# Graph attention kernel: rows loaded by SyncE as single tiles of 28 quads instead of as all tiles of 6 quads

## The chip, the cores and the metric

The kernel runs on one core of a Trainium2 chip. The metric is the device time of one execution in microseconds. A core has TensorE (PE in the profile; PEld is its weight load), VectorE (DVE), ScalarE (ACT), GpSimd (POOL) and SyncE (SP), each with an instruction queue of its own that runs in program order, and 16 DMA engines that they share.

## The reference

A graph with 6250 nodes and 206250 edges, sorted by receiver. Each edge has two feature vectors of 32 values, which pass through a small two-layer network each. Every node gets query, key and value rows of 128 values (8 heads of 16). Per edge and head, a score is the sum of query (receiver) times edge weight times key (sender); it scales the sender's value row, and the results are summed by receiver. The sum is added to the node's row and normalized.

```python
w_ij = silu(edge_feats @ rad_W1 + rad_b1) @ rad_W2 + rad_b2
w_ij = w_ij + silu(chi_scalar @ sph_W1 + sph_b1) @ sph_W2 + sph_b2
q_i = (x @ Wq)[receivers]
k_j = (x @ Wk)[senders]
alpha = (q_i * w_ij * k_j).reshape(-1, 8, 16).sum(-1) / sqrt(16) * cutoffs[:, None]
v_j = (x @ Wv)[senders].reshape(-1, 8, 16)
out = segment_sum(alpha[..., None] * v_j, receivers) / 16
return layernorm(x + out.reshape(-1, 128))
```

## The kernel before

**Tiles.** 128 edges are a tile, 4 tiles a quad (512 edges), 4 quads a group (2048 edges). There are 101 groups and 403 quads. `order` (L131) lists the quads as they are worked on: within a group 0, 2, 1, 3. Below, "quad i" is the i-th of that list.

**Prologue.** Key and value rows of all nodes are computed and written to a table `kv_tab` in HBM, 1 KB a node. For the first 10 quads the rows are computed from gathered node rows instead (L241). Then `rows_f` (L388 to L395) turns the sender numbers of chosen quads into byte addresses: VectorE multiplies by 1024, TensorE transposes, and `at_i` holds them as integers, a row of 128 per tile. `bias_rows`, the scaling of the edge weights and then `pick(0)` follow on VectorE in program order, and from `pick(0)` the first group's queries (`turn_q`, `make_q`) are made.

**The sender rows.** Every quad needs 512 rows of the table. Two ways lead there:
- `gathers` (L139), for nearly all quads: GpSimd issues four indirect DMAs, one a tile, each fetching 128 rows by the sender numbers in `src_i`. It is called 14 quads ahead (`AHEAD`). Each gather waits, by an added dependency, for a mark: one of the last four matmuls of `weigh` for quad i, where the gather is for quad i + 14.
- `load_rows` (L150), for 6 quads (`row_quads`, every 65th): SyncE issues 512 DMAs of one row each into a buffer `rows` (two of them). A unit is 16 rows: one instruction loads 16 addresses from `at_i` into registers (L163), then 16 DMAs follow (L167). The 32 units of a quad are spread over the quads before it; they must all be issued 8 quads ahead (`ROW_LEAD`).

**The main loop** (L666) runs over groups and four slots. In slot i TensorE sums messages of the group before (`sum_quads`), makes the first layers of quad i + 2, the queries at the edges of quad i + 1 and the edge weights (`weigh`) of quad i + 1. ScalarE applies the silu. VectorE does `multiply` for quad i + 1, then `scores` and `messages` for quad i.

**SyncE's queue** in one group, in this order: slot 0 an `x` load three groups ahead (a register load at L192 and a DMA at L195, behind a mark of TensorE), slot 2 the features `feats` of the group after next (L172, behind a mark of TensorE) and its relative receivers `relb` (L183), in every slot one `out` write (L624) if a row block is ready, and last in every slot `load_rows`. The writes of `out` overlap in rows, so one waits for the one before it. `feats` of a group is first read by TensorE's first layers two quads ahead of the group; `relb` by VectorE's `one_hots_T` (L432) in slot 1 of the group before.

**The order of work** is written out by hand; nothing moves an instruction within an engine's queue.

Of the kernel before, what the change touches and what calls it, by code (L numbers as in the profile page):

```python
# [12 lines left out]
F32 = mybir.dt.float32  # L13
BF16 = mybir.dt.bfloat16
U8 = mybir.dt.uint8
I32 = mybir.dt.int32
AF = mybir.ActivationFunctionType
OP = mybir.AluOpType
# [3 lines left out]
SP = mybir.EngineType.SP  # L22
WAIT = mybir.DependencyInfo(mybir.DependencyClass.Sync, mybir.DependencyReason.DATA)

P = 128
N = 6250
D = 128
HEADS = 8
HD = D // HEADS
# [3 lines left out]
QT = 4  # L33
# [4 lines left out]
EQ = P * QT  # L38
# [6 lines left out]
ROW_BYTES = 2 * D * 4  # L45
XQ = 10
RING = 16
ROW_QUADS = 6
ROW_LEAD = 8
ROW_UNIT = 16  # L50
CHECK = 20
XL = 3
NEIGHBORS = 16.0
# [5 lines left out]
def gnn_kernel(ctx, tc, x, src, dst, weight, edges, rad_W1, rad_b1, rad_W2, rad_b2,  # L59
# [14 lines left out]
    nc = tc.nc  # L74
    const = ctx.enter_context(tc.tile_pool(name="const", bufs=1))
# [8 lines left out]
    dst_i = const.tile([P, NT], I32, name="dst_i")  # L84
    src_i = const.tile([P, NT], I32, name="src_i")
    src_x = const.tile([P, math.ceil(XQ / NQ) * GT], I32, name="src_x")
    at_i = const.tile([ROW_QUADS * QT, P], I32, name="at_i")
    scale = const.tile([P, NT], F32, name="scale")
    w1 = const.tile([P, D], F32, name="w1")
    w2 = const.tile([P, 2, D], F32, name="w2")  # L90
# [5 lines left out]
    ident = const.tile([P, P], F32, name="ident")  # L96
# [16 lines left out]
    ep = ctx.enter_context(tc.tile_pool(name="edge", bufs=2))  # L113
# [7 lines left out]
    def quad_of(name, bufs, width=D):  # L121
        return ep.tile([P, QT, width], F32, name=name, bufs=bufs)

    def gather(o, table, index):
        return nc.gpsimd.indirect_dma_start(  # L125
            out=o, out_offset=None, in_=table,
            in_offset=bass.IndirectOffsetOnAxis(ap=index, axis=0))
# [1 line left out]


    order = [g * NQ + j for g in range(NG) for j in (0, 2, 1, 3) if g * NQ + j < QUADS]  # L131
    every = (len(order) - ROW_LEAD) // ROW_QUADS
    row_at = [(n + 1) * every for n in range(ROW_QUADS)]
    row_quads = {order[i] for i in row_at}
    r_of = {}
    feats_of, relb_of, act_of, kv_of, hot_of, hotT_of, x_of, q_of, msg_of = ({} for _ in range(9))
    po_of, part_of, to_of, tot_of, xT_of, y0_of, kq_of, pick_of, pq_of, pw_of = ({} for _ in range(10))

    def gathers(q, marks=()):  # L139

        if q in row_quads:
            return
        kv = quad_of("kv", RING, 2 * D)
        for t in range(QT):
            o = gather(kv[:, t, :], kv_tab, src_i[:, q * QT + t:q * QT + t + 1])
            if marks:
                tc.add_manual_dep(o.ins, marks[t].ins.name, WAIT, reason="no gather ahead of TensorE")
        kv_of[q] = kv

    def load_rows(i):  # L150

        k = max(i + ROW_LEAD - 1, 0) // every
        if k >= ROW_QUADS:
            return
        q, start = order[row_at[k]], max(k * every - ROW_LEAD + 1, 0)
        slots, units = row_at[k] - ROW_LEAD + 1 - start, EQ // ROW_UNIT
        a, b = ((j * units + slots - 1) // slots for j in (i - start, i - start + 1))
        if i == start:
            kv_of[q] = quad_of("rows", 2, 2 * D)
        table = kv_tab.bitcast(U8).rearrange("(o n) b -> o (n b)", o=1)  # L160
        for u in range(a, min(b, units)):
            t, e = u * ROW_UNIT // P, u * ROW_UNIT % P
            _, rows = nc.values_load_multi_w_load_instructions(  # L163
                at_i[k * QT + t:k * QT + t + 1, e:e + ROW_UNIT], engines=(SP,), min_val=0,
                max_val=(N - 1) * ROW_BYTES, skip_runtime_bounds_check_because="senders are nodes")
            for p in range(ROW_UNIT):
                nc.sync.dma_start(kv_of[q][e + p:e + p + 1, t, :].bitcast(U8),  # L167
                                  table[:, ds(rows[p], ROW_BYTES)])

    def load_feats(g, mark=None):  # L170
        feats_of[g] = gp.tile([P, EG // 2], F32, name="feats")
        o = nc.sync.dma_start(feats_of[g], edges[g])  # L172
        if mark is not None:
            tc.add_manual_dep(o.ins, mark.ins.name, WAIT, reason="one signal of TensorE a quad")
# [42 lines left out]
    with tc.tile_pool(name="nodes", bufs=1) as nodes, \  # L217
# [167 lines left out]
                nc.sync.dma_start(scale, weight)  # L385
        for q in order[XQ:AHEAD]:
            gathers(q)
        rows_f = nodes.tile([P, ROW_QUADS * QT], F32, name="rows_f")  # L388
        for k, i in enumerate(row_at):
            nc.vector.tensor_scalar(rows_f[:, k * QT:(k + 1) * QT],  # L390
                                    src_i[:, order[i] * QT:(order[i] + 1) * QT],
                                    float(ROW_BYTES), None, op0=OP.mult)
        pt = nps.tile([P, QT, P], F32, name="pt", bufs=3)
        nc.tensor.transpose(pt[:ROW_QUADS * QT, 0, :], rows_f, ident)
        nc.vector.tensor_copy(at_i, pt[:ROW_QUADS * QT, 0, :])  # L395
        nc.vector.tensor_tensor(bsum, b2[:, 0:1], b2[:, 1:2], op=OP.add)
        bias_rows()
        for t in range(P, NT, P):
# [5 lines left out]
    with tc.tile_pool(name="ps", bufs=1, space=PSUM) as pp:  # L404
# [57 lines left out]
        def after(o, mark, reason="one signal of TensorE a quad"):  # L462
            tc.add_manual_dep(o.ins, mark.ins.name, WAIT, reason=reason)

        def behind(o, marks, k):

            if marks:
                after(o, marks[k], "a signal of TensorE behind the quad's own")
# [16 lines left out]
        def weigh(q):  # L485

            pw = pp.tile([P, EQ], F32, name="pw", bufs=2)
            nc.tensor.matmul(pw, onesb, brow.rearrange("p t d -> p (t d)"), start=True, stop=False)  # L488
            pw = pw_of[q] = pw.rearrange("p (t d) -> p t d", d=D)
            marks = []  # L490
            for t in range(QT):
                for i in range(2):
                    o = nc.tensor.matmul(pw[:, t, :], act_of[q, i][:, t * P:(t + 1) * P], w2[:, i, :],  # L493
                                         start=False, stop=(t == QT - 1 and i == 1))
                    marks.append(o)
            return marks

        def multiply(q, mark=None, t=slice(0, QT)):
            if t.start == 0:
                kq_of[q] = quad_of("kq", 3)  # L500
            o = nc.vector.tensor_tensor(kq_of[q][:, t, :], pq_of[q][:, t, :], kv_of[q][:, t, :D],  # L501
                                        op=OP.mult)
            if mark is not None:
                after(o, mark)

        def scores(q, t=slice(0, QT), marks=()):
            n = t.stop - t.start
# [12 lines left out]
        def messages(q, alpha, t=slice(0, QT), marks=()):  # L520

            if t.start == 0:
                msg_of[q] = quad_of("msg", XQ)
            o = nc.vector.tensor_tensor(  # L524
                msg_of[q][:, t, :].rearrange("p t (h e) -> p t h e", e=HD),
                kv_of[q][:, t, D:].rearrange("p t (h e) -> p t h e", e=HD),
                alpha[:, :, :, None].to_broadcast([P, t.stop - t.start, HEADS, HD]), op=OP.mult)
            behind(o, marks, 3)

        def sum_quads(g, t, j=None):  # L530

            if g not in po_of:
                po_of[g] = pp.tile([P, D], F32, name="po")
            for j in range(NQ) if j is None else (j,):
                o = nc.tensor.matmul(po_of[g][j * W:(j + 1) * W, :], hot_of[g][:, j * QT + t, :],  # L535
                                     msg_of[g * NQ + j][:, t, :], start=(t == 0), stop=(t == QT - 1))
            return o

        wides = []

        def wide_one_hots(q):

            t = slice(q * QT, (q + 1) * QT)
            d = gp.tile([P, QT], F32, name="d", bufs=NQ)
            nc.vector.tensor_copy(d, dst_i[:, t])
            nc.vector.tensor_scalar(d, d, gb[:, q // NQ:q // NQ + 1], None, op0=OP.subtract)
            k = order[-3:].index(q)
            if k % 2 == 0:
                wides.append(quad_of("rows", 2, 2 * D).rearrange("p t (h r) -> p h t r", r=P))
            hot_of[q, "wide"] = wides[-1][:, k % 2]  # L550
            nc.vector.tensor_tensor(hot_of[q, "wide"], d[:, :, None].to_broadcast([P, QT, P]),
                                    colp[:, None, :].to_broadcast([P, QT, P]), op=OP.is_equal)

# [110 lines left out]
        marks = weigh(order[0])  # L664
        mark = marks[-1]
        for g in range(NG - 1):  # L666
            for slot, j in enumerate((0, 2, 1, 3)):
                q = g * NQ + j
                i = g * NQ + slot
# [9 lines left out]
                if 1 <= g:  # L679
                    for t in ((), (0, 1), (2,), (3,))[slot]:  # L680
                        mark = sum_quads(g - 1, t)
                first_layers(order[i + 2])
                mark = q_at_edges(order[i + 1])
                marks = weigh(order[i + 1])
# [32 lines left out]
                if g == NG - 2 and slot == 0:  # L717
                    wide_one_hots(order[-1])
                    n = nc.values_load(general, min_val=0, max_val=1)
# [7 lines left out]
        mark = q_at_edges(b)  # L727
        marks = weigh(b)
# [11 lines left out]
        mark = q_at_edges(c)  # L740
        marks = weigh(c)
# [195 lines left out]
```

## Time and profile before

| | |
|---|---|
| median of 3 runs | 2010.27 us (2009.23 to 2012.95) |
| the profiled execution's own time | 2011.89 us |
| its span, first to last instruction | 2010.1 us |
| mean granted clock of TensorE | 0.917 |
| gathers on GpSimd (table / nodes) | 1548 / 40 |
| rows issued by SyncE | 3072 of 1 KB |
| register loads of addresses on SyncE | 192 of 16 |

The profile page gives busy time by engine, the groups of instructions by source line, and the chain of waits followed back from the last instruction. A timeline line has start and duration in us, the engine, the line, the operation, what it writes and reads, how many were merged, and in brackets the idle time of the engine before it with what ended that. A line of a stretch has the stretch, its length, the busy time of the engine with its instructions, TensorE's granted clock, the DMA share and GB/s. Issuing instructions of SyncE are listed as SPq and do not count as busy time.

### The profile page before, as it was taken

To read this page: it belongs to the slowest core of one execution; us is meant where nothing else is said; L and a number is where in the kernel's file an instruction comes from. 1 tells how busy PE (TensorE), PEld (TensorE's weight loads), DVE (VectorE), ACT (ScalarE), POOL (GpSimd) and SP (SyncE) were. 2 spreads that over 40 slices of the span, in tenths; PEclk is the share of its full clock that TensorE was granted. 3 is DMA by queue.
4 is the path that set the end of the run, shared out by engine and by line. 5 is a ranking of instruction groups with operands and counts; after the bars stand their busy time and mean duration, and the time that the engine had idled before them with its cause. 6 is when DMAs were issued, how large, how long until landed. Compare 5 with 4: busy or idle time off the path is not lost.

```text
span 2010.1 us, 50508 instructions
## 1 busy us (share of the span) xinstructions
PE 1811.3 (90%) x16012; PEld 1519.6 (76%) x16012; DVE 1466.5 (73%) x3015; ACT 720.8 (36%) x1426; POOL 1505.3 (75%) x1596
## 2 busy tenths in 40 slices
PE   9898988999998988998998999988889889988897
PEld 7787877877877777777777777777777777777786
DVE  6687777878877776766767677767676776767687
ACT  2343333444343333333333332333332333323333
POOL 7777777777777777777777777777777777777775
PEclk9898988999998998998999889889998998898898
DMA  8454555555555555554554545554545555555553
GB/s 312 131 154 139 157 143 150 157 155 153 156 156 149 147 155 147 148 150 144 156 154 139 153 145 150 143 152 142 154 142 152 152 144 154 143 149 144 151 150 89
DMA packets 146414, 304.45 MB, mean 151 GB/s; under 512 B 36717, under 2 KB 79581, under 8 KB 146141
## 3 DMA queue, kind: packets, MB, share of 16 engines
q0 software_dynamic: 75584, 205.62, 36.6%
q1 hardware_dynamic: 69056, 95.15, 14.8%
q8 instruction: 127, 2.08, 0.4%
q14 instruction: 147, 1.20, 0.2%
q10 hardware_dynamic: 1500, 0.40, 0.1%
HBM read 287.58 MB, written 13.46 MB: 150 GB/s over the span
## 4 chain that ended last, share of the span: by engine, by line
PE 53%; DMA 20%; DVE 11%; issue 6%; ACT 4%; POOL 3%; SPq 2%; DVEq 0%; ACTq 0%; POOLq 0%
PE pw L493 27%; DMA kv<-kv_tab,src_i 17%; PE pq L457 10%; PE ph L446 7%; DVE kq L501 4%; PE po L535 4%; PE pw L488 2%; DMA feats<-in_edges 2%; DVE side L511 2%; DVE kq L509 2%; POOL msg L125 2%; POOL kv L125 1%; SPq L167 1%; ACT L478 1%; ACT y L612 1%
## 5 line engine op out<-in xcount | busy, mean ns | idle before, releaser
L125 POOL DMA_INDIRECT kv<-kv_tab,src_i x1548 | 1465.3, 947 | 474.3 <-PE pw L493 186.0
L478 ACT ACTIVATE act<-ph,b 128x512 f32<-128x512 f32 x806 | 518.4, 685 | 1150.5 <-PE pq L457 1124.0
L493 PE MATMUL pw<-w,act 128*128 128x128 f32 x6448 | 915.1, 300 | 0.0
L493 PEld LDWEIGHTS pw<-w,act 128*128 128x128 f32 x6448 | 834.8, 209 | 105.8 <-issue 93.9
L446 PE MATMUL ph<-feats,w 32*128 32x512 f32 x1612 | 497.2, 676 | 41.0 <-ACT act L478 20.9
L457 PE MATMUL pq<-q,hotT 32*128 32x128 f32 x3224 | 495.8, 296 | 42.6 <-DVE kq L501 42.6
L501 DVE TENSOR_TENSOR kq<-pq,kv 128x512 f32<-128x512 f32 x398 | 273.4, 687 | 331.9 <-DMA kv<-kv_tab,src_i 188.2
L457 PEld LDWEIGHTS pq<-q,hotT 32*128 32x128 f32 x3224 | 416.8, 198 | 79.9 <-issue 50.6
L511 DVE TENSOR_REDUCE side<-kq 128x32 f32<-128x512 f32 x404 | 280.2, 693 | 42.7 <-PE pw L493 0.9
L524 DVE TENSOR_TENSOR msg<-kv,side 128x512 f32<-128x512 f32 x398 | 273.2, 686 | 43.2 <-PE pq L457 0.9
L509 DVE TENSOR_TENSOR kq<-pw,kq 128x512 f32<-128x512 f32 x404 | 274.5, 679 | 0.1
L446 PEld LDWEIGHTS ph<-feats,w 32*128 32x128 f32 x1612 | 136.9, 193 | 123.8 <-issue 80.0
L488 PE MATMUL pw<-brow,onesb 3*128 3x512 bf16 x403 | 161.1, 400 | 0.0
L535 PE MATMUL po<-msg,hot 128*32 128x128 f32 x3200 | 155.7, 292 | 0.0
L574 PE MATMUL pq<-part,to 128*128 128x128 f32 x200 | 46.7, 317 | 82.9 <-DVE kq L501 58.4
L513 DVE TENSOR_TENSOR side<-side,scale 128x32 f32<-128x32 f32 x404 | 80.6, 200 | 42.6 <-DVE side L511 0.5
L574 PEld LDWEIGHTS pq<-part,to 128*128 128x128 f32 x200 | 31.9, 201 | 93.6 <-issue 57.4
L535 PEld LDWEIGHTS po<-msg,hot 128*32 128x32 f32 x3200 | 71.5, 111 | 38.9 <-issue 5.6
L432 DVE TENSOR_TENSOR hotT<-relb,side 128x512 f32<-128x512 bf16 x101 | 68.8, 682 | 34.0 <-DMA relb<-rel_lin 34.0
L437 DVE TENSOR_TENSOR hot<-rel,side 128x512 f32<-128x512 f32 x100 | 66.1, 661 | 0.0
L426 PE MATMUL pq<-wq,xT 128*128 128x128 f32 (+1 forms) x202 | 45.1, 308 | 15.2 <-DVE kq L501 14.4
L125 POOL DMA_INDIRECT msg<-in_x,src_x x40 | 39.0, 976 | 13.5 <-issue 11.6
(107 smaller groups left out, 839.3 us busy)
## 6 DMA issues: line engine op xcount, KB each, us to landing
feats<-in_edges SPq DMA_DIRECT2D x101, 512.0 KB
rows<-kv_tab SPq DMA_DIRECT2D x3072, 1.0 KB
kv<-kv_tab,src_i POOLq DMA_INDIRECT x1548
relb<-rel_lin SPq DMA_DIRECT2D x101, 128.0 KB
x<-in_x SPq DMA_DIRECT2D x101, 64.0 KB
out<-y SPq DMA_DIRECT2D x101, 64.0 KB
kv_tab<-kv SPq DMA_DIRECT2D x12, 512.0 KB
act<-in_x SPq DMA_DIRECT2D x12, 256.0 KB
```

The lines of the kernel that those rows point to most:

```text
L125: return nc.gpsimd.indirect_dma_start(out=o, out_offset=None, in_=table, in_offset=bass.IndirectOffsetOnAxis(ap=index, axis=0))
L446: return nc.tensor.matmul(act_of[q, i], w1[r0:r0 + R, :], feats_of[g][r0:r0 + R, c0:c0 + EQ], start=True, stop=True)
L457: o = nc.tensor.matmul(pq_of[q][:, t, :], hotT_of[g][b, t * P:(t + 1) * P], q_of[g][b, :], start=True, stop=True)
L478: o = nc.scalar.activation(act, act_of[q, i], AF.Silu, bias=b1[:, i:i + 1])
L488: nc.tensor.matmul(pw, onesb, brow.rearrange("p t d -> p (t d)"), start=True, stop=False)
L493: o = nc.tensor.matmul(pw[:, t, :], act_of[q, i][:, t * P:(t + 1) * P], w2[:, i, :], start=False, stop=(t == QT - 1 and i == 1))
L501: o = nc.vector.tensor_tensor(kq_of[q][:, t, :], pq_of[q][:, t, :], kv_of[q][:, t, :D], op=OP.mult)
L509: nc.vector.tensor_tensor(m, pw_of[q][:, t, :], m, op=OP.mult)
L511: o = nc.vector.tensor_reduce(alpha, m.rearrange("p t (h e) -> p t h e", e=HD), AX.X, OP.add)
L513: o = nc.vector.tensor_tensor(alpha, alpha, scale[:, q * QT + t.start:q * QT + t.stop, None].to_broadcast([P, n, HEADS]), op=OP.mult)
L524: o = nc.vector.tensor_tensor(msg_of[q][:, t, :].rearrange("p t (h e) -> p t h e", e=HD), kv_of[q][:, t, D:].rearrange("p t (h e) -> p t h ...
L535: o = nc.tensor.matmul(po_of[g][j * W:(j + 1) * W, :], hot_of[g][:, j * QT + t, :], msg_of[g * NQ + j][:, t, :], start=(t == 0), stop=(t = ...
```

## The change

Instead of all four tiles of 6 quads (24 tiles), SyncE loads the last tile of each of 28 quads (28 tiles), every 14th of the list. GpSimd gathers the other three tiles of those quads. A unit is 32 rows in place of 16, so a tile takes 4 units. The buffer of rows is a quarter of its size. In these quads `multiply` and `messages` run as two instructions each, three tiles from the gathered buffer and one from the other. The prologue makes 28 columns of addresses with one instruction each, where it made 24 with six. The one-hot tables of the last three quads, which used the buffer of rows, get one of their own.

```diff
-ROW_QUADS = 6
+ROW_TILES = 28
 ROW_LEAD = 8
-ROW_UNIT = 16
+ROW_UNIT = 32
...
-    every = (len(order) - ROW_LEAD) // ROW_QUADS
-    row_at = [(n + 1) * every for n in range(ROW_QUADS)]
+    every = (len(order) - ROW_LEAD) // ROW_TILES
+    row_at = [(n + 1) * every for n in range(ROW_TILES)]
...
     def gathers(q, marks=()):
-        if q in row_quads:
-            return
         kv = quad_of("kv", RING, 2 * D)
-        for t in range(QT):
+        for t in range(QT - 1 if q in row_quads else QT):
...
-        q, start = order[row_at[k]], max(k * every - ROW_LEAD + 1, 0)
-        slots, units = row_at[k] - ROW_LEAD + 1 - start, EQ // ROW_UNIT
+        slots, units = row_at[k] - ROW_LEAD + 1 - start, P // ROW_UNIT
         a, b = ((j * units + slots - 1) // slots for j in (i - start, i - start + 1))
         if i == start:
-            kv_of[q] = quad_of("rows", 2, 2 * D)
+            row_of[q] = ep.tile([P, 1, 2 * D], F32, name="rows", bufs=2)
-        for u in range(a, min(b, units)):
-            t, e = u * ROW_UNIT // P, u * ROW_UNIT % P
+        for e in range(a * ROW_UNIT, min(b, units) * ROW_UNIT, ROW_UNIT):
             _, rows = nc.values_load_multi_w_load_instructions(
-                at_i[k * QT + t:k * QT + t + 1, e:e + ROW_UNIT], engines=(SP,), min_val=0,
+                at_i[k:k + 1, e:e + ROW_UNIT], engines=(SP,), min_val=0,
...
+    def kv_parts(q, t):
+        if q not in row_quads:
+            return [(t, kv_of[q][:, t, :])]
+        return [(slice(0, QT - 1), kv_of[q][:, :QT - 1, :]), (slice(QT - 1, QT), row_of[q])]
...
-        rows_f = nodes.tile([P, ROW_QUADS * QT], F32, name="rows_f")
+        rows_f = nodes.tile([P, ROW_TILES], F32, name="rows_f")
         for k, i in enumerate(row_at):
-            nc.vector.tensor_scalar(rows_f[:, k * QT:(k + 1) * QT],
-                                    src_i[:, order[i] * QT:(order[i] + 1) * QT],
+            c = order[i] * QT + QT - 1
+            nc.vector.tensor_scalar(rows_f[:, k:k + 1], src_i[:, c:c + 1],
                                     float(ROW_BYTES), None, op0=OP.mult)
...
-            o = nc.vector.tensor_tensor(kq_of[q][:, t, :], pq_of[q][:, t, :], kv_of[q][:, t, :D],
-                                        op=OP.mult)
+            for u, kv in kv_parts(q, t):
+                o = nc.vector.tensor_tensor(kq_of[q][:, u, :], pq_of[q][:, u, :], kv[:, :, :D],
+                                            op=OP.mult)
...
-            if k % 2 == 0:
-                wides.append(quad_of("rows", 2, 2 * D).rearrange("p t (h r) -> p h t r", r=P))
-            hot_of[q, "wide"] = wides[-1][:, k % 2]
+            hot_of[q, "wide"] = quad_of("wide", 3, P)
```

The units of a tile are spread over the 14 slots between two such quads, and for the first tile over the first 7 slots of the loop: its four units stand in slots 0, 1, 3 and 5, and those of the second in 7, 10, 14 and 17. Before, the first quad's 32 units were spread over 58 slots.

More of the change, by code (lines that the diff above doesn't have):

```diff
@@ L86, in gnn_kernel @@
     src_x = const.tile([P, math.ceil(XQ / NQ) * GT], I32, name="src_x")
-    at_i = const.tile([ROW_QUADS * QT, P], I32, name="at_i")
+    at_i = const.tile([ROW_TILES, P], I32, name="at_i")
     scale = const.tile([P, NT], F32, name="scale")
@@ L131, in gnn_kernel @@
     order = [g * NQ + j for g in range(NG) for j in (0, 2, 1, 3) if g * NQ + j < QUADS]
-    every = (len(order) - ROW_LEAD) // ROW_QUADS
-    row_at = [(n + 1) * every for n in range(ROW_QUADS)]
+    every = (len(order) - ROW_LEAD) // ROW_TILES
+    row_at = [(n + 1) * every for n in range(ROW_TILES)]
     row_quads = {order[i] for i in row_at}
+    row_of = {}
     r_of = {}
@@ L152, in load_rows @@
         k = max(i + ROW_LEAD - 1, 0) // every
-        if k >= ROW_QUADS:
+        if k >= ROW_TILES:
             return
         q, start = order[row_at[k]], max(k * every - ROW_LEAD + 1, 0)
-        slots, units = row_at[k] - ROW_LEAD + 1 - start, EQ // ROW_UNIT
+        slots, units = row_at[k] - ROW_LEAD + 1 - start, P // ROW_UNIT
         a, b = ((j * units + slots - 1) // slots for j in (i - start, i - start + 1))
         if i == start:
-            kv_of[q] = quad_of("rows", 2, 2 * D)
+            row_of[q] = ep.tile([P, 1, 2 * D], F32, name="rows", bufs=2)
         table = kv_tab.bitcast(U8).rearrange("(o n) b -> o (n b)", o=1)
-        for u in range(a, min(b, units)):
-            t, e = u * ROW_UNIT // P, u * ROW_UNIT % P
+        for e in range(a * ROW_UNIT, min(b, units) * ROW_UNIT, ROW_UNIT):
             _, rows = nc.values_load_multi_w_load_instructions(
-                at_i[k * QT + t:k * QT + t + 1, e:e + ROW_UNIT], engines=(SP,), min_val=0,
+                at_i[k:k + 1, e:e + ROW_UNIT], engines=(SP,), min_val=0,
                 max_val=(N - 1) * ROW_BYTES, skip_runtime_bounds_check_because="senders are nodes")
             for p in range(ROW_UNIT):
-                nc.sync.dma_start(kv_of[q][e + p:e + p + 1, t, :].bitcast(U8),
+                nc.sync.dma_start(row_of[q][e + p:e + p + 1, 0, :].bitcast(U8),
                                   table[:, ds(rows[p], ROW_BYTES)])
+    def kv_parts(q, t):
+        if q not in row_quads:
+            return [(t, kv_of[q][:, t, :])]
+        return [(slice(0, QT - 1), kv_of[q][:, :QT - 1, :]), (slice(QT - 1, QT), row_of[q])]
     def load_feats(g, mark=None):
@@ L387, in gnn_kernel @@
             gathers(q)
-        rows_f = nodes.tile([P, ROW_QUADS * QT], F32, name="rows_f")
+        rows_f = nodes.tile([P, ROW_TILES], F32, name="rows_f")
         for k, i in enumerate(row_at):
-            nc.vector.tensor_scalar(rows_f[:, k * QT:(k + 1) * QT],
-                                    src_i[:, order[i] * QT:(order[i] + 1) * QT],
+            c = order[i] * QT + QT - 1
+            nc.vector.tensor_scalar(rows_f[:, k:k + 1], src_i[:, c:c + 1],
                                     float(ROW_BYTES), None, op0=OP.mult)
         pt = nps.tile([P, QT, P], F32, name="pt", bufs=3)
-        nc.tensor.transpose(pt[:ROW_QUADS * QT, 0, :], rows_f, ident)
-        nc.vector.tensor_copy(at_i, pt[:ROW_QUADS * QT, 0, :])
+        nc.tensor.transpose(pt[:ROW_TILES, 0, :], rows_f, ident)
+        nc.vector.tensor_copy(at_i, pt[:ROW_TILES, 0, :])
         nc.vector.tensor_tensor(bsum, b2[:, 0:1], b2[:, 1:2], op=OP.add)
@@ L500, in multiply @@
                 kq_of[q] = quad_of("kq", 3)
-            o = nc.vector.tensor_tensor(kq_of[q][:, t, :], pq_of[q][:, t, :], kv_of[q][:, t, :D],
-                                        op=OP.mult)
-            if mark is not None:
-                after(o, mark)
+            for u, kv in kv_parts(q, t):
+                o = nc.vector.tensor_tensor(kq_of[q][:, u, :], pq_of[q][:, u, :], kv[:, :, :D],
+                                            op=OP.mult)
+                if mark is not None:
+                    after(o, mark)
         def scores(q, t=slice(0, QT), marks=()):
@@ L523, in messages @@
                 msg_of[q] = quad_of("msg", XQ)
[L524 to L528, printed above, removed]
+            for u, kv in kv_parts(q, t):
+                n = u.stop - u.start
+                o = nc.vector.tensor_tensor(
+                    msg_of[q][:, u, :].rearrange("p t (h e) -> p t h e", e=HD),
+                    kv[:, :, D:].rearrange("p t (h e) -> p t h e", e=HD),
+                    alpha[:, u.start - t.start:u.stop - t.start, :, None].to_broadcast(
+                        [P, n, HEADS, HD]), op=OP.mult)
+                behind(o, marks, 3)
         def sum_quads(g, t, j=None):
@@ L537, in sum_quads @@
             return o
-        wides = []
         def wide_one_hots(q):
@@ L546, in wide_one_hots @@
             nc.vector.tensor_scalar(d, d, gb[:, q // NQ:q // NQ + 1], None, op0=OP.subtract)
-            k = order[-3:].index(q)
-            if k % 2 == 0:
-                wides.append(quad_of("rows", 2, 2 * D).rearrange("p t (h r) -> p h t r", r=P))
-            hot_of[q, "wide"] = wides[-1][:, k % 2]
+            hot_of[q, "wide"] = quad_of("wide", 3, P)
             nc.vector.tensor_tensor(hot_of[q, "wide"], d[:, :, None].to_broadcast([P, QT, P]),
```

## The prediction

> **What bounds the kernel now.** I read the page first, then GpSimd's timeline, then the same engine by stretches, then SyncE's queue.
>
> ```profile
> PE 1811.3 (90%) x16012; PEld 1519.6 (76%) x16012; DVE 1466.5 (73%) x3015; ACT 720.8 (36%) x1426; POOL 1505.3 (75%) x1596
> PE 53%; DMA 20%; DVE 11%; issue 6%; ACT 4%; POOL 3%; SPq 2%; DVEq 0%; ACTq 0%; POOLq 0%
> L125 POOL DMA_INDIRECT kv<-kv_tab,src_i x1548 | 1465.3, 947 | 474.3 <-PE pw L493 186.0
> ```
>
> By busy shares and by the chain of waits TensorE bounds it. But the 1548 gathers have 474.3 us of idle time before them, 0.306 us each, and it is the same before nearly every one (first GpSimd's timeline, then its busy time and number of instructions by stretch):
>
> ```profile
> 73.88 0.94 POOL L125 DMA_INDIRECT kv<-kv_tab,src_i  x1 [0.30 <-issue]
> 77.60 0.94 POOL L125 DMA_INDIRECT kv<-kv_tab,src_i  x1 [2.78 <-PE pw L493]
> ...
> 1992.76 0.95 POOL L125 DMA_INDIRECT kv<-kv_tab,src_i  x1 [0.30 <-issue]
> ```
>
> ```profile
> 80.00:340.00 260.00, 196.72 (x208) 0.91 0.51 148
> 1400.00:1800.00 400.00, 302.47 (x320) 0.92 0.51 148
> ```
>
> A gather is 0.95 us and the 0.30 us belong to it: one starts every 1.25 us in every stretch (208 in 260 us, 320 in 400 us). The timeline has one longer wait after the first gather, 2.78 us at 77.60, for the mark of TensorE's first `weigh`. So GpSimd is full from 3.2 to 1993.7 us, and 16.4 us of tail follow. TensorE and VectorE are quicker: they start 14 quads behind the gathers, win that back until about 600 us, and then wait for rows that have just landed.
>
> While they win it back, SyncE decides (SyncE's queue, then TensorE and VectorE behind it):
>
> ```profile
> 80.23 11.78 SPq L167 DMA_DIRECT2D rows<-kv_tab  x32
> 92.12 0.37 SPq L172 DMA_DIRECT2D feats<-in_edges  x1
> ...
> 120.82 5.11 SPq L167 DMA_DIRECT2D rows<-kv_tab  x16
> ...
> 128.71 6.31 SPq L167 DMA_DIRECT2D rows<-kv_tab  x16
> ...
> 162.83 12.74 SPq L167 DMA_DIRECT2D rows<-kv_tab  x32
> ...
> 183.07 0.37 SPq L172 DMA_DIRECT2D feats<-in_edges  x1
> ```
>
> ```profile
> 187.26 1.22 PE L446 MATMUL ph<-feats,w 32*128 32x512 f32 x2 [6.70 <-DMA feats<-in_edges]
> 189.20 0.69 DVE L432 TENSOR_TENSOR hotT<-relb,side 128x512 f32<-128x512 bf16 x1 [7.94 <-DMA relb<-rel_lin]
> 189.66 3.78 PE L493 MATMUL pw<-w,act 128*128 128x128 f32 x16
> ```
>
> Its queue runs without a gap from 80 to 600 us. Where three units of 16 rows fell between two loads of `feats`, that load came late (183.07, after 160.15), TensorE stood still 6.70 us and VectorE 7.94 us. `feats` is usable about 4.6 us after its issue, `relb` 5.8. After such a stop the 16 matmuls of `weigh` took 3.78 us; running on, they take 2.05.
>
> **The change part by part.**
>
> *Gathers.* 24 leave the list before, 28 after: 4 fewer, 4 x 1.25 = -5.0 us on the bound engine.
>
> *Preparation.* 28 multiplications for `rows_f` instead of 6. The six took 0.52 us at 0.154 each, so their starts are 0.073 apart: 22 x 0.073 = +1.6 us (bounds 0 and 22 x 0.154 = 3.4). VectorE runs without a pause from there to `pick(0)` at 67.12, on which `turn_q`, `make_q` and the first `weigh` hang, and GpSimd is already waiting for that: nothing hides it. +1.6.
>
> *VectorE.* In 28 quads `multiply` and `messages` become two instructions each. A 128x128 one takes 0.28 us, 128x256 0.41, 128x512 0.69, so a pair costs some 0.15 us more; 56 x 0.15 = 8 us, spread over the run and covered by the 188 us that `multiply` waits for gathers; without that cover 8 us.
>
> *SyncE, each row.* 512 more rows, at (5.11 - 0.23)/15 = 0.325 us each. The loads of registers become 112 of 32 in place of 192 of 16:
>
> ```profile
> L163 SPq TENSOR_LOAD <-at_i x192: 972/1179/1674, 78.7 to 1896.4; - x192
> L192 SPq TENSOR_LOAD <-gb_i x101: 268/543/793, 25.7 to 1920.7; - x101
> 209.94 3.93 SPq L624 DMA_DIRECT2D out<-y  x2
> ```
>
> Both kinds depend on what stands before them, but compared like with like (after rows 0.545 and 1.248; after `relb` 0.773 and 1.524) 15 more registers cost 0.70 to 0.75 us. So 32 cost 0.77 more than 16, 1.76 to 2.28 us. Bounds: no more than now (1.18), and two loads of 16 (2.5). I take 0.77. The Trainium skill (Runtime: NRT & Kernel Launch, Instruction fetch mechanics) puts such a load at about 200 ns a register, 6.4 us for 32. By that 16 would take 3.2 us; the row has 1.18, so the row decides.
>
> *SyncE, the start.* This is the large term. The first tile now has 7 slots for 128 rows, units of 32 in slots 0, 1, 3 and 5; before, 32 rows lay ahead of the first `feats` of the loop and 32 more ahead of the second (109.00). Counted on from 78.6, where the third `x` has been issued: unit 0, 2.4 to its first row and 10.3 for 32 rows (31 x 0.325 + 0.23); unit 1, 2.2 + 10.3; `feats` and `relb` 1.1; unit 2, behind `relb`, 2.4 + 10.3 + 1.3 (6.31 less 5.11 and a little); `x` 1.1; unit 3, 2.1 + 10.3. Sum 53.7: `feats(3)` leaves at 132.3 instead of 109.0. TensorE's first layer of quad 12 starts at 136.9 and, slow after the stop, gives the mark of `weigh(11)` to GpSimd 5.4 us later (as after the stop at 187.26, where five of its eight steps were done at 189.66 + 5/8 x 3.78 = 192.0, 4.8 us on; and the 0.6 that GpSimd took to start at 77.60), at 142.3. GpSimd, free to run, would come to quad 25 at 77.60 + 43 x 1.25 = 131.4 (3 gathers for quad 14, 40 for 15 to 24). It waits **10.9 us**; behind it in its queue are all other gathers. The same sum to `feats(6)`, with two units in slots 14 and 17: three times (1.1 + 14.0 + 1.1), one `out` 0.5, 12.4, is 61.5 us; GpSimd needs 47 x 1.25 = 58.8 for quads 25 to 36, so **2.7 us** more. Bounds for both together: 0 (margin larger than counted) and 20 (the four loads 0.6 dearer, the delay after a stop doubled).
>
> *SyncE, the long run.* In 28 quads (7 groups, two tiles): 256 x 0.325 = 83.2; 8 loads with the way to the first row, four at 2.42 and four at 1.90, 17.3; stalls behind `relb` 4 x 1.3 + 3 x 0.5 = 6.7; `x`, `feats` with `relb`, `out` 7 x 2.7 = 19.1; waits of an `out` for the one before it, which no unit separates any longer in some groups (at 209.94 two `out` took 3.93 us; behind `relb` the wait was 5), 7.4. Sum 133.7 us. GpSimd needs 110 x 1.25 = 137.6. So SyncE stays below, by 3%: the 14 quads are hardly won back. From `feats(6)` at 195.4 it takes 13 x 133.7 = 1738 us to the last `feats` with rows ahead, at 1933.5; `relb` is there at 1939.8, and from that `one_hots_T` (quad 385) the rest takes 15.2 us for four quads when VectorE runs without a pause, 16.1 for the next four (1943.30 to 1959.44 in the trace) and 50.7 from there to the end, less 1.1 that it waited for a gather there: 81 us, the end at 2020.8.
>
> *The sum.* By GpSimd: -5.0 + 1.6 + 10.9 + 2.7 = +10.2 us. On the profiled execution (span 2010.1, own time 2011.89) that is a span of 2020.3; on the median of the runs, 2010.27, 2020.5. That run's own time would be 2022.1. By SyncE the end is at 2020.8 of the span, 2021.0 on the median. The later of the two holds: **2021**.
>
> **The rivals.**
>
> *SyncE becomes the bound.* For: 133.7 against 137.6 is within what I can miss. Each us more per 28 quads is 13 us at the end: at 136, 2050; with loads at twice those of 16, about +50, 2070. Against: at 1.18 to 1.2 us for 16 the line through the loads is straight. Time 2028 to 2070. Chance 0.32.
>
> *The late loads don't reach GpSimd, and the shorter list counts.* The place is the wait at quad 25: it vanishes if `feats(3)` leaves 11 us sooner than counted, at 121 (units that cost 10 instead of 13 us each). Then 2010.27 - 5.0 + 1.6 = 2006.9, and 2005.3 if the preparation is hidden too. For: GpSimd's period is rigid and stalls of up to 7.94 us cost nothing before. Against: they fell at 189 us, when the margin had grown to some 20 us; at quad 25 it was about 15 (first gather at 132.6, mark at about 117). Chance 0.15.
>
> *A load that grows faster with its registers.* Beyond twice those of 16 SyncE alone paces the kernel, above 2070. The skill's figure above would make it some 2500. Chance 0.02; nothing in the rows shows it.
>
> **How the numbers follow.** Forecast 0.51 (2014.5 to 2028), and the three rivals. What can't be told from no change is 0.2%, 4.0 us. Faster by more is half of the second rival, 0.08; within it the other half and the forecast's lower edge, 0.08; slower 0.84. The range takes in the second rival's upper value and the first up to 2060: 2006 to 2060, leaving out some 0.15; the forecast's own range is 2014.5 to 2028.
>
> **What would show it.** Right: waits of GpSimd of several us for `pw` near 110 to 145 us and again near 200; `feats` issues at about 92 + 13 and 134 us; SyncE's loads at 1.7 to 2.3 us; a queue of SyncE without gaps far beyond 600 us; 1544 gathers at 1.25. Wrong: no wait of GpSimd beyond the first (then about 2007), or a load far above 2.3 us; or SyncE without a gap up to 1900 us and a tail of 25 us or more behind the last gather, which would be the first rival.

## The result and the profile after

The changed kernel takes 2020.55 us (median of 6 runs, 2017.47 to 2025.67) against 2010.36 us (6 runs, 2009.23 to 2012.95) for the one before on the same chip: a ratio of 1.0053, 95% interval 1.0041 to 1.0065. It is slower by 10 us. Its profiled execution took 2022.82 us, with a span of 2021.0 and a mean granted clock of 0.906.

The page of the kernel after (busy time, the chain of waits by engine, three groups):

```profile
PE 1739.1 (86%) x16012; PEld 1479.3 (73%) x16012; DVE 1466.4 (73%) x3093; ACT 718.5 (36%) x1426; POOL 1500.5 (74%) x1592
PE 51%; SPq 15%; DMA 11%; DVE 10%; issue 7%; ACT 3%; POOL 2%; DVEq 0%; ACTq 0%; POOLq 0%
L125 POOL DMA_INDIRECT kv<-kv_tab,src_i x1544 | 1460.9, 946 | 486.5 <-PE pw L497 201.5
L450 PE MATMUL ph<-feats,w 32*128 32x512 f32 x1612 | 502.2, 680 | 226.1 <-DMA feats<-in_edges 200.0
L436 DVE TENSOR_TENSOR hotT<-relb,side 128x512 f32<-128x512 bf16 x101 | 69.0, 683 | 247.1 <-DMA relb<-rel_lin 247.0
```

TensorE is busy 72 us less than before and the kernel is slower: busy time says nothing of the cause. SyncE's queue now holds 15% of the chain (2% before). TensorE waited 200.0 us for `feats` and VectorE's `one_hots_T` 247.0 us for `relb`; in the trace of before these waits were 20.1 and 34.0 us.

GpSimd's timeline: the gathers of the main loop with a wait other than the usual 0.30 us, and the last one:

```profile
78.76 0.94 POOL L125 DMA_INDIRECT kv<-kv_tab,src_i  x1 [4.59 <-PE pw L497]
...
114.74 0.94 POOL L125 DMA_INDIRECT kv<-kv_tab,src_i  x1 [2.52 <-PE pw L497]
...
142.63 0.94 POOL L125 DMA_INDIRECT kv<-kv_tab,src_i  x1 [8.23 <-PE pw L497]
...
202.94 0.94 POOL L125 DMA_INDIRECT kv<-kv_tab,src_i  x1 [1.75 <-PE pw L497]
...
1999.96 0.95 POOL L125 DMA_INDIRECT kv<-kv_tab,src_i  x1 [0.30 <-PE pq L461]
```

The same engine by stretches:

```profile
80.00:340.00 260.00, 188.05 (x199) 0.88 0.48 140
340.00:600.00 260.00, 196.60 (x209) 0.94 0.51 149
1400.00:1800.00 400.00, 302.44 (x321) 0.91 0.51 150
```

The first gather behind the start waits until 78.76 (77.60 before). Three more waits follow, at quads 21, 25 and 37, of 2.22, 7.93 and 1.45 us beyond 0.30, 11.6 us in all. They cost about nine gathers of the first stretch (199 for 208 before, with room for one at an edge), and from 340 us on the period of 1.25 us is back. Those gathers are never made good, since GpSimd has no spare time.

SyncE's queue at the start and at the end of the row loads, in the kernel after:

```profile
82.25 22.89 SPq L165 DMA_DIRECT2D rows<-kv_tab  x64
105.58 0.37 SPq L176 DMA_DIRECT2D feats<-in_edges  x1
...
109.33 10.34 SPq L165 DMA_DIRECT2D rows<-kv_tab  x32
...
122.81 10.77 SPq L165 DMA_DIRECT2D rows<-kv_tab  x32
133.68 0.37 SPq L176 DMA_DIRECT2D feats<-in_edges  x1
...
194.23 0.37 SPq L176 DMA_DIRECT2D feats<-in_edges  x1
...
1921.55 10.41 SPq L165 DMA_DIRECT2D rows<-kv_tab  x32
1932.06 0.37 SPq L176 DMA_DIRECT2D feats<-in_edges  x1
```

What TensorE waited for behind the first two `feats` of the loop:

```profile
109.57 1.22 PE L450 MATMUL ph<-feats,w 32*128 32x512 f32 x2 [9.16 <-DMA feats<-in_edges]
...
137.45 1.22 PE L450 MATMUL ph<-feats,w 32*128 32x512 f32 x2 [9.86 <-DMA feats<-in_edges]
```

And what VectorE waited for behind the last of these loads, with the loads of registers as a group (shortest, median and longest in ns):

```profile
1937.77 0.69 DVE L436 TENSOR_TENSOR hotT<-relb,side 128x512 f32<-128x512 bf16 x1 [9.96 <-DMA relb<-rel_lin]
```

```profile
L161 SPq TENSOR_LOAD <-at_i x112: 1868/2140/2561, 79.8 to 1919.4; - x112
```

Two units ahead of `feats(2)` put it at 105.58, 13.5 us later than before, and two more put `feats(3)` at 133.68, 24.7 us later. TensorE stood 9.16 and 9.86 us for them, its `weigh` came late, and GpSimd stood 2.52 and 8.23 us for the marks, at 114.74 and 142.63. That it hangs together this way is tested below.

How far `multiply` of a quad starts after the quad's last gather began shows whether the gathers or SyncE set the pace (worked out from the timelines, us):

| quad | 10 | 52 | 94 | 122 | 248 | 318 | 374 | 402 |
|---|---|---|---|---|---|---|---|---|
| before | 53.4 | 40.1 | 21.5 | 4.4 | 3 to 5 | 3 to 5 | 3 to 5 | 3 to 5 |
| after | 67.6 | 58.2 | 51.9 | 43.7 | 34.3 | 24.1 | 7.1 | 7.4 |

Before, the gathers set the pace from quad 122 on. After, the work stays behind them until the run is nearly over: SyncE sets the pace of TensorE and VectorE all along, but it is quicker than GpSimd. From `feats(6)` at 194.23 to `feats(97)` at 1932.06 it takes 133.7 us per 28 quads, GpSimd 137.6.

### The profile page after: what moved, and what is told of

It is laid out like the page before. It is cut to its first block, busy times and chain, and to the rows that moved or that the text cites. A ratio compares the mean times of both kernels' runs of the same rounds, so it can differ in the third digit from the quotient of the medians.

```text
span 2021.0 us, 51553 instructions
## 1 busy us (share of the span) xinstructions
PE 1739.1 (86%) x16012; PEld 1479.3 (73%) x16012; DVE 1466.4 (73%) x3093; ACT 718.5 (36%) x1426; POOL 1500.5 (74%) x1592
## 4 chain that ended last, share of the span: by engine, by line
PE 51%; SPq 15%; DMA 11%; DVE 10%; issue 7%; ACT 3%; POOL 2%; DVEq 0%; ACTq 0%; POOLq 0%
PE pw L497 26%; SPq L165 12%; PE pq L461 9%; PE ph L450 7%; DMA feats<-in_edges 5%; PE po L543 3%; SPq L161 3%; PE pw L492 2%; DVE kq L506 2%; DMA kv<-kv_tab,src_i 2%; DVE side L516 2%; DVE kq L514 2%; POOL msg L125 2%; ACT L482 1%; DMA out<-y 1%
## 5 line engine op out<-in xcount | busy, mean ns | idle before, releaser
L497 PEld LDWEIGHTS pw<-w,act 128*128 128x128 f32 x6448 | 819.2, 206 | 112.4 <-issue 101.8
L497 PE MATMUL pw<-w,act 128*128 128x128 f32 x6448 | 899.0, 297 | 0.0
L506 DVE TENSOR_TENSOR kq<-pq,kv 128x512 f32<-128x512 f32 (+1 forms) x404 | 272.7, 675 | 130.3 <-PE pq L461 104.4
L531 DVE TENSOR_TENSOR msg<-kv,side 128x512 f32<-128x512 f32 (+1 forms) x404 | 273.7, 677 | 43.6 <-DVE side L518 1.9
L436 DVE TENSOR_TENSOR hotT<-relb,side 128x512 f32<-128x512 bf16 x101 | 69.0, 683 | 247.1 <-DMA relb<-rel_lin 247.0
L125 POOL DMA_INDIRECT msg<-in_x,src_x x40 | 38.5, 964 | 13.3 <-issue 11.6
L615 ACT ACTIVATE y<-y,shift,rs 128x128 f32<-128x128 f32 x100 | 41.5, 482 | 15.8 <-DVE shift L611 14.9
```

Of the source, the lines that this page charges most:

```text
L125: return nc.gpsimd.indirect_dma_start(out=o, out_offset=None, in_=table, in_offset=bass.IndirectOffsetOnAxis(ap=index, axis=0))
L506: o = nc.vector.tensor_tensor(kq_of[q][:, u, :], pq_of[q][:, u, :], kv[:, :, :D], op=OP.mult)
L531: o = nc.vector.tensor_tensor(msg_of[q][:, u, :].rearrange("p t (h e) -> p t h e", e=HD), kv[:, :, D:].rearrange("p t (h e) -> p t h e", e ...
```

## The experiments

The first four ran on one chip beside the kernel before (median 2010.44 us of 19 runs). Each trace is one execution, and those of one kernel differ by a few us: the changed kernel's trace took 2.3 us more than its median, that of the first tile later 1.9 less, that with units of 16 5.5 less. My theory: the crowded start of SyncE's queue reaches GpSimd and costs some 13 us, SyncE then wins back little; the shorter list of gathers gives 5 us. Rivals: the more numerous VectorE instructions cost the 10 us; or SyncE's total of work does.

**The first tile later** (`e1_first_tile_later`). The rows begin with quad 28 instead of 14, so 27 tiles in all, and the first tile has 21 slots for its units instead of 7.

```diff
-ROW_TILES = 28
+ROW_TILES = 27
...
-    every = (len(order) - ROW_LEAD) // ROW_TILES
-    row_at = [(n + 1) * every for n in range(ROW_TILES)]
+    every = (len(order) - ROW_LEAD) // (ROW_TILES + 1)
+    row_at = [(n + 2) * every for n in range(ROW_TILES)]
...
-        k = max(i + ROW_LEAD - 1, 0) // every
+        k = max((i + ROW_LEAD - 1) // every - 1, 0)
...
-        q, start = order[row_at[k]], max(k * every - ROW_LEAD + 1, 0)
+        q, start = order[row_at[k]], (row_at[k - 1] - ROW_LEAD + 1 if k else 0)
```

> 27 tiles, the first of them in quad 28 in place of quad 14, so that its four units stand in slots 0, 5, 10 and 15 and not in 0, 1, 3 and 5; the rest as in the change. Theory (rows of SyncE delay feats and relb, and GpSimd waits for the marks of quads 7, 11 and 23): no wait of GpSimd beyond the first at about 79 us, feats of the groups 2 and 3 back before 95 and 115 us; three gathers fewer than before, -3.75, preparation +1.2, a tail up to 3 us longer: 2007 to 2012, about 2009.5. Rival (56 more instructions on VectorE cost it): 2018 or more. Rival (the load of 32 addresses is too dear everywhere): 2016 or more.

Measured: 2009.24 us (10 runs, 2007.39 to 2012.56), ratio 0.9996 (0.9986 to 1.0005). GpSimd's timeline and SyncE's queue in it:

```profile
78.37 0.95 POOL L125 DMA_INDIRECT kv<-kv_tab,src_i  x1 [4.02 <-PE pw L497]
...
1988.92 0.95 POOL L125 DMA_INDIRECT kv<-kv_tab,src_i  x1 [0.30 <-issue]
```

```profile
82.24 10.42 SPq L165 DMA_DIRECT2D rows<-kv_tab  x32
92.76 0.37 SPq L176 DMA_DIRECT2D feats<-in_edges  x1
...
97.20 10.79 SPq L165 DMA_DIRECT2D rows<-kv_tab  x32
108.10 0.37 SPq L176 DMA_DIRECT2D feats<-in_edges  x1
```

With one unit ahead of each `feats`, `feats(3)` leaves at 108.10, as before, and behind the first wait of GpSimd only one of 0.45 us is left. The last gather starts 11.0 us sooner than in the changed kernel, with the 27 other tiles, the units of 32 and the split instructions all in place. So the crowded start costs these 11 us. One tile less also takes work off SyncE, but the waits that went all stood in the first tenth of the run, before 203 us. The lag is 28.5 us at quad 52, 16.1 at 122 and about 5 at 234: it falls by 23.5 us in 182 quads, 3.6 us per 28, close to the 137.6 less 133.7 that the prediction counted.

**The split alone** (`e3_split_only`). The kernel before, with `multiply` and `messages` cut in two in every 14th quad.

```diff
+    split = {order[(n + 1) * 14] for n in range(28)}
...
+    def parts(q, t):
...
+        if q not in split:
+            return [t]
+        return [slice(0, QT - 1), slice(QT - 1, QT)]
...
-            o = nc.vector.tensor_tensor(kq_of[q][:, t, :], pq_of[q][:, t, :], kv_of[q][:, t, :D],
-                                        op=OP.mult)
+            for u in parts(q, t):
+                o = nc.vector.tensor_tensor(kq_of[q][:, u, :], pq_of[q][:, u, :],
+                                            kv_of[q][:, u, :D], op=OP.mult)
...
```

> The kernel before, with multiply and messages split in three tiles and one in every 14th quad, and nothing else of the change. Theory: about 8 us of VectorE's time spread over the run, all of it inside its waits for gathers: 2008.5 to 2012. Rival (the split is what costs): 2016 to 2020.

Measured: 2012.65 us (10 runs, 2011.44 to 2013.68), ratio 1.0008 (0.9999 to 1.0018). That is a little above the expected 2008.5 to 2012; the rival of 2016 or more falls, but a cost of up to 0.18%, 3.6 us, is not excluded. What covers the split here, `multiply`'s 188 us of waits for gathers, is 19.8 us in the changed kernel. There VectorE's 247.0 us of waits for `relb` can cover it; this was not tested apart, but the run with the first tile later holds 27 of the splits and is level with the kernel before.

**Units of 16 in the changed kernel** (`e4_unit16`): `ROW_UNIT = 16`, 224 loads of registers instead of 112. It makes SyncE's work larger, spreads it in finer pieces and leaves the rest.

> The change with units of 16 rows, so 224 loads of 16 addresses in place of 112 of 32, and finer pieces. Theory (SyncE's total is what counts): loads some 4 us more per 28 quads, less a few us of waits of out, and the first tile some 6 us later: 2020 to 2045, about 2027. Rival (the long units and their dear loads are the cost): 2016 or less.

Measured: 2068.7 us (2063.25 to 2073.25), ratio 1.0295 (1.0277 to 1.0312). The direction is the theory's, the range too low. Its loads of registers, the last `feats` with rows ahead, `feats(97)`, and GpSimd's last gather:

```profile
L161 SPq TENSOR_LOAD <-at_i x224: 971/1233/1672, 81.1 to 1981.3; - x112
```

```profile
1975.14 0.37 SPq L176 DMA_DIRECT2D feats<-in_edges  x1
```

```profile
2007.67 0.94 POOL L125 DMA_INDIRECT kv<-kv_tab,src_i  x1 [0.30 <-DMA kv<-kv_tab,src_i]
```

Two loads of 16 take 2.47 us where one of 32 takes 2.14, and row issues stood behind a `relb` in 73 places for 56.1 us (21 places and 8.8 us with units of 32); the waits of one `out` for another shrank from 123.0 to 81.2 us. That is (112 x 0.33 + 47 - 42)/13, some 3.2 us more per 28 quads. The queue shows 3.4: from `feats(6)` at 193.19 to `feats(97)` at 1975.14 it takes 137.1 us per 28 quads instead of 133.7, all but level with GpSimd's 137.6. So the lag is hardly won back: it falls from 63.7 us at quad 52 to 42.1 at quad 402. GpSimd stands eleven times beyond its first wait, 18 us in all, and behind the start of its last gather 53.8 us follow. This is the prediction's first rival, "SyncE becomes the bound", and its price holds: 13 us for each us per 28 quads is 44 us here, and the span is 40.5 us longer (2061.5). 2.5% of SyncE's time lay between the changed kernel and it, and units of 32 are what keeps the changed kernel on the right side. My expectation counted about 4 us more per 28 quads but carried too little of it to the end: 4 x 13 is 52 us already.

**A remedy that failed** (`e2_feats_by_scalar`). From the third group on, `feats` and `relb` are issued by ScalarE's queue, so that no row stands ahead of them.

```diff
-        o = nc.sync.dma_start(feats_of[g], edges[g])
+        o = (nc.sync if g < 2 else nc.scalar).dma_start(feats_of[g], edges[g])
...
-        nc.sync.dma_start(relb_of[g], r[:, None, :].to_broadcast([NQ, W, EQ]))
+        (nc.sync if g < 2 else nc.scalar).dma_start(relb_of[g], r[:, None, :].to_broadcast([NQ, W, EQ]))
```

> The change, but feats and relb of the groups from 2 on are issued by ScalarE's queue in place of SyncE's. Theory: nothing that TensorE needs soon stands behind rows any longer; no waits of GpSimd at 115, 143 and 203 us, hotT and the first layers hardly wait, the lag behind the gathers is gone by 700 us and the tail is 16.4 us again: -5.0 + 1.2, so 2005.5 to 2008.5. Rival (56 more instructions on VectorE): 2014 or more. Rival (the load of 32 addresses is too dear in itself): above 2012.

Measured: 2581.5 us (2570.42 to 2589.12), ratio 1.2822 (1.2779 to 1.2865). The expectation was wrong by 570 us. Its waits, then two units of rows on SyncE's queue:

```profile
PE pq L420 <- DMA x<-in_x: 655.7, 96, 22.4
```

```profile
941.61 17.83 SPq L165 DMA_DIRECT2D rows<-kv_tab  x32
960.19 0.36 SPq L199 DMA_DIRECT2D x<-in_x  x1
962.63 19.76 SPq L165 DMA_DIRECT2D rows<-kv_tab  x32
```

The waits for `relb` are gone, as meant. But 32 rows now take 17.83 and 19.76 us instead of 10.4: SyncE's row issues waited 747.9 us in 98 places, once a group, for a `feats` that ScalarE's queue had started. `x`, still behind the rows, came late for that (655.7 us of TensorE), and the mean granted clock fell to 0.814. Why rows on one queue wait while the large transfer of another runs was not settled; the run only shows that moving it cost more than its place in the queue.

**Runs in which the gathers didn't bind.** The other eight ran on three chips on which the kernel before took 2660 us (medians 2659.02 to 2660.16) at a granted clock of 0.80 to 0.82. There TensorE stands idle with nothing shown that it waits for, and GpSimd waits for TensorE all along (1071.8 us idle before the gathers in the first of them, where 1548 x 0.30 would be 464). What a wait of GpSimd costs can't be seen on them, so they tell nothing of the theory, except where a cost on another engine is concerned. These chips are behind from the start: `feats(0)` leaves at 81.11 us in the first of these runs and at 38.01 in the kernel before on the first chip, before any row is loaded.

The kernel before with `ROW_UNIT = 32` (`e5_before_unit32`):

> The kernel before, with units of 32 rows in its 6 quads and nothing else. Theory (SyncE's total and the start decide): 96 loads of about 2.1 us in place of 192 of 1.24, some 40 us less for SyncE; the lag behind the gathers ends earlier than at 600 us, the gathers set the end: 2009 to 2012. Rival (long units delay feats and so the end): 2014 or more.

Measured: 2661.99 against 2659.91 us, ratio 1.0006 (0.9995 to 1.0017). From its page:

```profile
L125 POOL DMA_INDIRECT kv<-kv_tab,src_i x1548 | 1467.2, 948 | 1071.8 <-PE pw L493 442.0
```

A gather is still 0.95 us; it is the marks of TensorE that come late. Before TensorE's own weight loads for the first layers (215.1 us in 312 places) and for `make_q` (206.0 us in 77) the releaser is "issue", that is, none.

The 28 address columns by two strided instructions (`e6_two_instructions`), and rows in every 13th quad from 26 on, 29 tiles (`e7_every13`):

```diff
-        for k, i in enumerate(row_at):
-            c = order[i] * QT + QT - 1
-            nc.vector.tensor_scalar(rows_f[:, k:k + 1], src_i[:, c:c + 1],
+        for h in range(2):
+            c = [order[i] * QT + QT - 1 for i in row_at[h::2]]
+            gap = c[1] - c[0]
...
+            nc.vector.tensor_scalar(rows_f[:, h::2], src_i[:, c[0]:c[-1] + 1:gap],
...
```

> The change, with the 28 columns of addresses made by two instructions with a stride in place of 28. Theory (the preparation is on the path to the first mark): 26 starts of 0.05 to 0.07 us less, GpSimd's first wait ends 1.2 to 1.9 us earlier, at about 77.2 us, and everything behind it with it: 2018.5 to 2019.8. Rival (the preparation is hidden): 2020.5 and the first wait ends at 78.8.

> As the run with the later first tile, but 29 tiles, every 13th quad from quad 26 on: 1543 gathers, five fewer than before. Theory (SyncE's total is within 3% of the gathers' pace in the change, and a tile costs it about 53 us): SyncE is now the bound, the lag is not won back and a tail of 50 us or more stands behind the last gather: 2050 to 2080, about 2070. Rival (a shorter list of gathers always counts once the start is mended): 2004 to 2008.

Measured: 2655.47 (0.9986, 0.9977 to 0.9996) and 2643.77 us (0.9942, 0.9922 to 0.9963). The first is the changed kernel but for the preparation; that it is level with the kernel before, or 0.1% quicker, fits a change whose cost lies in the gathers' waits, which don't bind here. Whether 29 tiles overload SyncE, as I expected, stays untested.

No row loads at all, so that the messages of 28 tiles are missing from the sums, in three separate runs on three chips (`e8_no_rows`, `e9_no_rows_again`, `e12_no_rows_third`):

> The change without any row loads of SyncE: the last tile of the 28 quads is read from one buffer of zeros, so the messages of those tiles are left out of the sums. The split instructions, the 28 preparations and the 1544 gathers stay. Theory: no wait of GpSimd beyond the first and a tail of 16.4 us: 2010.4 - 5.0 + 1.2, so 2005.5 to 2007.5. Rival (the split on VectorE takes part): 2010 or more.

Measured: 2591.37, 2586.04 and 2590.0 us, ratios 0.9741 (0.9723 to 0.976), 0.9753 (0.9718 to 0.9788) and 0.9744 (0.9726 to 0.9762). Without the rows the kernel is 2.5% quicker on these chips although the gathers don't bind, and 2.4% quicker than the changed kernel with its rows on the same chip (2591.37 for 2655.47). TensorE's wait at "issue" before `make_q` is 164.0 us with rows (`e11_late_lead10`) and 18.9 without (`e12_no_rows_third`); what lies behind it is open.

Two attempts at a better version, both with 27 tiles from quad 28 and two preparing instructions: one in which ScalarE's queue writes `out` (`e10_late_out_by_scalar`), one with `ROW_LEAD = 10` (`e11_late_lead10`).

> The run with the later first tile (27 tiles from quad 28 on), the addresses made by two instructions, and out written from ScalarE's queue for all but the last five groups, so that SyncE no longer waits for one out behind another. Theory: SyncE gains 1.2 to 1.8 us a group, the lag is gone early, the tail is 16.4 us: -3.75 - 0.3 on the kernel before, 2005 to 2007.5. Rival (a transfer from ScalarE's queue holds up the rows as feats did, or ScalarE is held by the wait for the out before): 2012 or more.

> The run with the later first tile (27 tiles from quad 28 on), the addresses made by two instructions, and every row two quads earlier, so that the last two units between two loads of feats stand 16 quads earlier and not at the end. Theory: 1545 gathers, the first wait 0.3 shorter than in the kernel before, a tail of 16.4 us in every run: 2010.4 - 3.75 - 0.3, so 2005 to 2008.5. Rival (the rest of the later-tile run's time is not SyncE's last delay): 2009 or more.

Measured: 2797.87 us, ratio 1.0529 (1.0514 to 1.0543), and 2659.12 us, 0.9996 (0.9987 to 1.0006). With `out` on the other queue SyncE's rows waited for its transfers (88.2 us in 15 places) and TensorE's weight loads of the first layers waited 358.7 us at "issue": the second time that a transfer on ScalarE's queue cost more than it freed. No run showed a version that beats both kernels. The nearest, the first tile later, is level with the one before.

## Why the prediction was right, step by step

**What bounds.** GpSimd's rigid period was the point to see, against busy shares and chain. It held: 1544 gathers at 1.25 us, and every us that GpSimd stood early is lost at the end.

**Gathers and preparation.** 4 gathers fewer, -5.0. For the preparation 1.6 was counted; the gather behind the first wait starts 1.16 us later.

**Loads of registers.** 32 addresses were put at 0.77 above 16, 1.76 to 2.28. Measured 1.87 to 2.56, median 2.14 for 1.18: 0.96 more, and some 0.9 when those behind the same transfer are compared (behind `x` 1.92 for 1.00, behind `relb` 2.40 for 1.51). That lies inside the bounds of "no more than now" and "two loads of 16". The Trainium skill (Runtime: NRT & Kernel Launch, Instruction fetch mechanics) puts a register at about 200 ns, by which 32 would take an estimated 6.4 us. The trace doesn't agree; the page speaks of loads from HBM, and these come from on-chip memory. The rival built on a load that grows faster falls.

**VectorE's split** was counted as hidden: 1.0008 (0.9999 to 1.0018) in the kernel before bears it out within 3.6 us.

**The start.** `feats(3)` was put at 132.3 + 1.6 = 133.9 and left at 133.68; `feats(6)` at 195.4 and left at 194.23. The wait at quad 25 was 10.9 in the prediction; it came as two, 2.22 at quad 21 and 7.93 at quad 25, 10.15 together. That part of it would come four quads sooner the prediction did not see, though its sum holds `feats(2)`: at 105.58, behind two units, it already held up the mark. The sum to quad 25 is the same either way. Near 200 us it was 2.7, measured 1.45. One term is too large in both: 4.6 us from the issue of `feats` to TensorE's first use of it. The prediction's own lines give 4.2 (183.07 to 187.26), the trace after 3.8 and 3.5 (133.68 to 137.45, 194.23 to 197.77). The first tile moved later removed all of these.

**SyncE's long run.** 133.7 us per 28 quads put the last `feats` behind rows at 1933.5; it left at 1932.06, thirteen rounds on, and the measured round is 133.7 too (in the sum, 7 x 2.7 is 18.9 and not 19.1). `relb` released `one_hots_T` at 1937.77 instead of 1939.8, 2.0 us sooner; the rest took 83.2 us for 81, 2.2 longer. The end: 2021.0 of the span for 2020.8. That the two misses cancel is luck, and so is an end that fits to 0.2 us when the runs of this kernel lie between 2017.47 and 2025.67; the round of 133.7 is not.

**Which account holds.** The prediction had two, 2020.3 by GpSimd and 2020.8 by SyncE, and let the later hold. This was needed, since GpSimd's term was about 3 us too large. The last gather starts 7.20 us later than before (1999.96 for 1992.76), where 10.2 were counted. The waits and the preparation as measured give -5.0 + 1.16 + 11.6 = 7.8. Of the 3 us, 1.25 are in the wait near 200 us, 0.75 in the one at quad 25, 0.4 in the preparation, and 0.6 in small differences of the period. But behind the start of the last gather come 21.0 us instead of 17.3, because `one_hots_T` still waited 9.96 us for `relb` at 1937.77: 7.2 + 3.7 is the 10.9 us of the span. By GpSimd's account alone the span would have been about 2017. That SyncE's remaining delay makes the 3.7 us is read from the trace; in the run with the first tile later, where the lag was gone, 16.7 us followed.

**The rivals.** "SyncE becomes the bound" didn't happen at units of 32 and did at 16, which sets its point: at 133.7 us per 28 quads the lag is all but won back by the end and costs 3.7 us, at 137.1 it is not. "The late loads don't reach GpSimd" needed `feats(3)` to leave 11 us sooner; the run in which it left at 108.10 shows that mechanism, with 2009.24 us, 2.3 above the 2006.9 that was counted for it (it also has one gather more, 1.25 us; the rest is within the spread of its runs, 2007.39 to 2012.56).

## What to carry to other kernels

An engine whose instructions each have the same short idle time before them, in every stretch, is full, whatever its busy share; then look for what makes it stand still even once, for it can't make that good. Work that is spread out evenly over a run is harmless only where the queue has room: put nothing of it into the start, where the engines behind the queue have the least margin. When two engines come to nearly the same end by count, work out both and take the later one.

## What the runs showed of the hardware

- A load of registers on SyncE from on-chip memory takes 0.54 us (median; 0.27 to 0.79) for one, 1.18 for 16 and 2.14 for 32. It is shorter behind an `x` than behind a `relb` (medians of 32: 1.92 and 2.40).
- With `feats` (512 KB) and `relb` started on ScalarE's queue, single-row issues of SyncE's queue stood 7.6 us for a `feats` each time (747.9 us in 98 places), and the kernel was 28% slower.
- The same kernel took 2010 us on one chip and 2660 on three others, at a lower granted clock (0.80 to 0.82 for 0.915 to 0.929). A gather took the same 0.95 us on both (there in the run with units of 32). A low clock is not these chips' alone: on the first chip the run with `feats` on ScalarE's queue was granted 0.81 to 0.82. Without rows on SyncE the kernel was 2.5% quicker on the three. The cause wasn't found.
